# A convolution-attention and mixture-of-experts kernel: pieces of a visit over four PSUM slots, and image 0's sorting spread one operation to a step

## The chip, the cores and the metric

The kernel runs on one core of a Trainium2 chip. The metric is the device time of one execution in microseconds (us). Besides the time of several plain executions there is one execution with the hardware profiler on; its trace gives every instruction's start, duration and wait. Of the engines, TensorE (PE in the profile) multiplies matrices into PSUM, VectorE (DVE) and ScalarE (ACT) work on the elements and copy PSUM results to SBUF, which is called evicting here, GpSimd (POOL) does some element work and issues indirect DMAs, and SyncE (SP) issues most of the other DMAs.

## What is computed

The input x has the shape (2, 256, 56, 56) in float32: two images of 256 channels and N = 3136 positions. All arithmetic is in float32. The reference, cut to what matters:

```python
x = conv_attention(x)              # non-local block over the positions, no softmax, then relu(wy + x)
t = tokens(x)                      # (2, 3136, 256)
t = t + attention(layer_norm(t))   # 4 heads of 64, causal, softmax, projection W_proj
xf = layer_norm(t)
probs = softmax(xf @ gate_w + gate_b)          # 8 experts
top2_vals, top2_idx = top_k(probs, 2)
for e in range(8):                             # hidden width 512
    out += weight(e) * (gelu(xf @ W1[e] + b1[e]) @ W2[e] + b2[e])
x = image(t + out)
```

The reference evaluates every expert for every token; the kernel sorts the tokens by expert and evaluates the two chosen ones.

## The kernel before

**Stages.** The convolution part comes first (to about 92 us). Then layer norm and attention run (92 to about 867 us), image 0 and then image 1. Then the expert stage works through blocks of 128 token places (slots), and the rows are combined and stored.

**Attention.** The queries of an image are cut into 7 bands i of 448, the heads into two pairs hp. A step takes one band, one pair and one block j of 128 keys; there are 200 steps in an image, of some 1.5 us each. A step does `scores` of step n (line 721, into one of two score tiles of two PSUM banks, pool `psc`), the exponential on ACT (729) into a tile `st` (five buffers), on blocks that the diagonal cuts a mask on DVE (731), the running row sums `acc` on DVE (743), and `values` of step n - 3 (761, tile `yp`).

**Visits.** After the last step of a band and pair comes a visit. It does pieces of later work on TensorE: `query_key` (603, evicted by ACT at 611), `value` (618, evicted by ACT at 627; at the end of a segment DVE scales gate columns at 638), `transpose` (589, evicted by ACT at 595) of layer-normed rows, and up to two pairs of output projections (`project_out`, 671, added to the tokens t by DVE at 676, then the mean and variance of the new rows, `stats`, 177 and 178). Every piece takes a PSUM bank from `bank()`, which hands out the two banks of pool `pm` in turn. After the pieces `sum_rows` (785) adds up `acc` over partitions, also in a bank of `pm`.

**The queue.** Beside the visits every step calls `between`, which pulls work from a list of generators, `queue`: on every second step it pulls two pieces. `pull` goes through the generators in their order, and stops at the first that answers True (something was done); one that answers False is passed over, and the next one gets its turn. For each image b there is a generator `tokens(b)`: the output projections of 25 tiles in pairs (which wait for their queries to be finished, and answer "pe" so that a visit takes them up), and then `dispatch(b)`: inverse deviations by Newton steps (1041 to 1053), router and top two experts (1056 and after), rank of each token among its expert's (1122), places, one-hot vectors (1236), and at last, for each tile of 128 tokens, the normalised row `xr` (DVE, 1355; for image 1 also 1361) and two indirect DMAs by POOL that scatter it into `x_slots` (1363). `tokens(0)` then loads the experts' first weights and the first rows. Image 1's generator comes behind image 0's in the queue.

**Experts.** The expert stage takes 102 blocks in its main loop. Each has a transpose (1462), the first product `hidden` (1485), Gelu on ACT (1494), and, three blocks later in order, the second product `outputs` (1504), evicted by DVE (1514, tile `ys`, three buffers). DVE copies the weights of the block two ahead (1473). The blocks run in the order of their slots, image 0's first; blocks 42 to 44 are the first that hold both images' rows. Rows come three blocks to a load, `fetch`: the loads for block n + 6 are issued when block n begins (SP, 1403, and 1415 for the second image's part), and DVE makes them ready three blocks later (1428 to 1439). `fetch` first calls `need(b)`, which pulls the queue without pause until all of image b's rows have been sent. Between blocks `meanwhile` pulls two or three pieces. SP and every other engine run their instructions in the order of the program; `y_slots` (1519) is stored by SP behind `fetch`.

The parts of the code that the change touches:

Of the kernel before, what the change touches and what calls it, by code (L numbers as in the profile page):

```python
# [28 lines left out]
def conv_attn_moe_kernel(  # L29
# [52 lines left out]
    P = 128  # L82
# [429 lines left out]
    def layer1(nm, general):  # L512

        with ExitStack() as whole:
# [4 lines left out]
            bg = pool(whole, "bg", bufs=2)  # L519
            g1 = pool(whole, "g1", bufs=1)  # L520

            def bank(name, shape=(P, 512)):
                return pm.tile(list(shape), F32, tag="m", name=f"{name}_{nm}")

            def centre_gate(place):
# [135 lines left out]
            def project_out(b, qT, done):  # L661

                for first, m, k in pairs():
                    while done() < (first + m - 1) * P + k:
                        yield False
                    yield "pe"
                    for n in range(first, first + m):
                        o = n * P
                        ps = bank(f"pp_{b}_{n}")
                        for c in range(NH):  # L670
                            nc.tensor.matmul(  # L671
                                ps[:k, : C + E], qT[:, c, o : o + k], wpr[:, c, :],
                                start=(c == 0), stop=(c == NH - 1),
                            )
                        t = ts[b][:k, n, : C + E]
                        nc.vector.tensor_tensor(t, t, ps[:k, : C + E], ALU.add)
                        if b == 0:
                            nc.sync.dma_start(out=rest_d[:k, n], in_=t[:, :C])
                    stats(b, first, m, k, bg, f"o{nm}{b}")

                    for _ in range(3 if b else 1):
                        yield True

            def attend(
                b, qT, kT, v, fst, fs, psc, py, visit, between, clock, later, finished
# [145 lines left out]
                for n in range(len(steps) + LAG):  # L831
                    if 0 < n <= len(steps) and steps[n - 1][4]:
                        i, hp = steps[n - 1][:2]
                        visit(i, hp)
                        sum_rows(hp, i)
                    if n < len(steps):
                        i = steps[n][0]
                        between(i, ends[i] - n)

                    late = n >= LAG and steps[n - LAG][3]  # L840
                    if n >= LAG:
                        due(clock[0])
# [161 lines left out]
            def dispatch(b):  # L1004

                t = ts[b]
                tail = chunk(NCH - 1)
                ops = [0]

                def small_piece():  # L1010

# [17 lines left out]
                def wide(ap):  # L1029
# [8 lines left out]
                    small(k, 1).rearrange("p t o -> p (t o)") for k in ("newton_x", "newton_y", "red")  # L1038
                )
                nc.vector.tensor_scalar(x, var, 1e-5, None, ALU.add)  # L1040
                nc.vector.tensor_scalar(
                    y.bitcast(I32), x.bitcast(I32), 1, None, ALU.arith_shift_right
                )
                nc.vector.tensor_scalar(
                    y.bitcast(I32), y.bitcast(I32), -1.0, float(0x5F3759DF), ALU.mult, ALU.add
                )
                yield from small_piece()
                for i in range(4):
                    to = var if i == 3 else y
                    nc.vector.tensor_tensor(z, y, y, ALU.mult)  # L1050
                    nc.vector.tensor_tensor(z, z, x, ALU.mult)
                    nc.vector.tensor_scalar(z, z, -0.5, 1.5, ALU.mult, ALU.add)
                    nc.vector.tensor_tensor(to, y, z, ALU.mult)
                    yield from op()
                    yield from small_piece()
# [294 lines left out]
                for n in range(NCH):  # L1350
                    kk = chunk(n)
                    xr = (scatter_rows[0] if b else bg).tile(
                        [P, width], F32, tag="xr", name=f"xr_{nm}{b}_{n}"
                    )
                    nc.vector.tensor_scalar(
                        xr[:kk, :C], t[:kk, n, :C],
                        t[:kk, n, MEAN : MEAN + 1], t[:kk, n, RSTD : RSTD + 1],
                        ALU.subtract, ALU.mult,
                    )
                    if b:  # L1360
                        nc.vector.tensor_copy(xr[:kk, C:], t[:kk, n, C + E - 2 : SLOT + 1])  # L1361
                    for k in range(2):
                        s = nc.gpsimd.indirect_dma_start(  # L1363
                            out=xds[b],
                            out_offset=bass.IndirectOffsetOnAxis(ap=idxs[b][:kk, k, n : n + 1], axis=0),
                            in_=xr[:kk],
                            in_offset=None,
                            bounds_check=xds[b].shape[0] - 1,
                            oob_is_err=False,
                        )  # L1370
                        group = f"x_slots_{nm}{b}"
                        tc.declare_no_dep(s.ins, group=group, reason="different rows")
                        tc.add_to_no_dep_group(group, s.ins)
                        if b or k:
                            yield True
                    if b == 0:
                        yield False
                sent[b] = True

            def experts(w1s, w2s, b2s, ex, es, ps6, between, need, written, settle, decide):  # L1380
# [538 lines left out]
            else:  # L1919
                fst = pool(att, "fst", bufs=5)  # L1920
                fs = pool(end, "fs", bufs=2, side="right")
                psc = pool(att, "psc", bufs=2, space=PSUM)
                py = pool(att, "py", bufs=1, space=PSUM)
                projections = [project_qkv(b, qT, kT, v, px) for b in range(B)]
                finished = [[0] * NH for b in range(B)]
# [37 lines left out]
                for b in range(B):  # L1963
                    queue.append(tokens(b, qT, lambda b=b: min(finished[b])))

                    def visit(i, hp):

                        now, then = ahead(b, i, hp)
                        for piece in now:
                            piece()  # L1970
                        for _ in range(2):
                            pull()
                            products()
                        for piece in then:
# [12 lines left out]

                    due = attend(
                        b, qT, kT, v, fst, fs, psc, py, visit, between,
# [252 lines left out]
```

## Time and profile before

| | us |
|---|---|
| time, median of 3 runs | 1326.75 (1324.08 to 1327.43) |
| the profiled execution's own time | 1320.51 |
| its span in the trace | 1318.7 |
| TensorE busy | 1269.1 (96%) |
| VectorE busy | 798.3 (61%) |
| ScalarE busy | 610.9 (46%) |
| GpSimd busy | 348.8 (26%) |
| attention: first visit to the first expert block | 92 to 867 |
| first expert block to the end | 867 to 1318.7 |

The mean clock that was granted to TensorE is 0.991 of full speed. Lines in the profile are those of the kernel before. A row of the waits names the waiting instruction and what it was released by, its total in us, the number of waits and the longest one. A row of the timeline has the start in us from the span's start, the duration, the engine, the line, the operation, output and inputs, and in brackets the engine's idle time ahead of it with its releaser. Ends of matmuls are modelled, so that part of a wait can be counted as busy time of the matmul before it; starts are measured.

### The profile page before, as it was taken

Reading aid. Unit: us, or ns where it says so; the run is one execution under the profiler, and the core shown is the slowest. Engines: PE = TensorE matmul, PEld = TensorE weight load, DVE = VectorE, ACT = ScalarE, POOL = GpSimd, SP = SyncE. Lnnn points to the kernel's source line nnn. Section 1 sums busy time; section 2 is a strip of 40 time slices with the busy share of each in tenths; the row PEclk is TensorE's granted clock in tenths of the full one; section 3 lists DMA queues with packets and bytes.
Section 4 is the critical chain, followed back from the end, with each engine's and each line's share of the span. In section 5 each row is a group of like instructions: output and inputs, shape, how many; then the busy total and the mean of one; then the engine's idle time right before and its main releaser. Section 6 shows DMA issues by size and latency. Waiting matters only on the chain.

```text
span 1318.7 us, 28564 instructions
## 1 busy us (share of the span) xinstructions
PE 1269.1 (96%) x10809; PEld 827.2 (63%) x10809; DVE 798.3 (61%) x1673; ACT 610.9 (46%) x1235; POOL 348.8 (26%) x319
## 2 busy tenths in 40 slices
PE   9999999999999999999999999999998999899997
PEld 8875445544444555444444444579987899799996
DVE  1673566666777745756877777754753443355554
ACT  0255555556566544555655455633432333344432
POOL 1113330000002223311126620000066312665551
PEclk9999999999999999999999999999999899999999
DMA  9994100000000001000002243321234343466654
GB/s 317 359 349 129 31 16 24 25 17 16 17 9 8 25 1 37 18 11 9 16 24 81 81 133 95 105 72 53 69 128 147 117 113 94 139 195 193 189 162 132
DMA packets 111074, 123.88 MB, mean 94 GB/s; under 512 B 19703, under 2 KB 100840, under 8 KB 110930
## 3 DMA queue, kind: packets, MB, share of 16 engines
q1 hardware_dynamic: 100130, 95.18, 23.7%
q0 software_dynamic: 9840, 25.67, 5.7%
q8 instruction: 89, 1.46, 0.5%
q10 hardware_dynamic: 960, 1.11, 0.3%
q14 instruction: 55, 0.45, 0.1%
HBM read 62.06 MB, written 61.05 MB: 93 GB/s over the span
## 4 chain that ended last, share of the span: by engine, by line
PE 87%; DVE 6%; ACT 3%; issue 3%; DMA 1%; POOL 0%; SPq 0%; DVEq 0%; ACTq 0%; POOLq 0%
PE sc_f L721 18%; PE yp_f L761 18%; PE ht_f L1485 14%; PE yp_f L1504 13%; PE qk_f L603 7%; PE v_f L618 3%; PE cp L410 3%; DVE acc_f L743 2%; PE gram L317 2%; PE pp_f L671 2%; ACT st_f L729 2%; PE tp_f L1462 2%; PE sp_f L785 1%; PE yo_f L1727 1%; DMA out_dram<-ot_f 1%
## 5 line engine op out<-in xcount | busy, mean ns | idle before, releaser
L729 ACT ACTIVATE st_f<-sc_f 128x896 f32<-128x896 f32 (+5 forms) x400 | 330.4, 840 | 225.0 <-PE sc_f L721 199.3
L743 DVE TENSOR_TENSOR acc_f<-acc_f,st_f 128x896 f32<-128x896 f32 (+5 forms) x372 | 379.9, 1021 | 74.0 <-ACT st_f L729 62.2
L721 PE MATMUL sc_f<-qT_f,kT_f 64*64 64x448 f32 (+6 forms) x3184 | 340.6, 500 | 9.4 <-ACT st_f L729 6.0
L761 PE MATMUL yp_f<-st_f,v_f 64*64 64x448 f32 (+6 forms) x3184 | 339.9, 501 | 3.5 <-DVE st_f L731 2.3
L1494 ACT ACTIVATE g_f<-ht_f,b1b 128x128 f32<-128x128 f32 x408 | 116.5, 370 | 252.0 <-PE ht_f L1485 125.1
L721 PEld LDWEIGHTS sc_f<-qT_f,kT_f 64*64 64x64 f32 x3184 | 121.0, 133 | 164.5 <-issue 124.2
L761 PEld LDWEIGHTS yp_f<-st_f,v_f 64*64 64x64 f32 x3184 | 120.0, 133 | 154.3 <-issue 131.7
L1485 PE MATMUL ht_f<-xT_f,w_f 128*128 128x128 f32 x1632 | 206.4, 280 | 4.5 <-issue 3.6
L1485 PEld LDWEIGHTS ht_f<-xT_f,w_f 128*128 128x128 f32 x1632 | 201.7, 196 | 11.3 <-issue 6.0
L773 POOL TENSOR_TENSOR qT_f<-both_f 128x448 f32<-128x448 f32 x28 | 37.0, 1321 | 503.0 <-ACT both_f L772 503.0
L1363 POOL DMA_INDIRECT x_slots<-xr_f,idx x100 | 110.0, 1100 | 144.0 <-DVE xr_f L1361 100.8
L1473 DVE COPY w_f<-w1s_f 128x1024 f32 x102 | 72.7, 714 | 84.8 <-PE ht_f L1485 37.7
L574 POOL TENSOR_SCALAR xn_f<-t 128x256 f32<-128x256 f32 (+1 forms) x50 | 80.8, 1624 | 155.3 <-PE xp_f L589 66.2
L1525 POOL DMA_INDIRECT y_tokens<-ys_f,to_f x57 | 59.0, 1036 | 126.1 <-DVE ys_f L1514 102.3
L1514 DVE TENSOR_TENSOR ys_f<-yp_f,kT_f 128x128 f32<-128x128 f32 x102 | 29.5, 289 | 102.8 <-PE yp_f L1504 72.8
L603 PE MATMUL qk_f<-px_f,wat 128*128 128x512 f32 (+2 forms) x224 | 88.5, 547 | 0.8 <-ACT px_f L595 0.6
L603 PEld LDWEIGHTS qk_f<-px_f,wat 128*128 128x128 f32 x224 | 40.5, 190 | 46.2 <-issue 41.1
L739 DVE COPY acc_f<-st_f 128x896 f32<-128x896 f32 x28 | 17.9, 641 | 80.1 <-ACT st_f L729 76.3
L1504 PE MATMUL yp_f<-v_f,g_f 128*128 x204 | 62.2, 385 | 2.0 <-issue 1.9
L731 DVE TENSOR_TENSOR st_f<-st_f,keep 128x256 f32<-128x256 f32 (+1 forms) x112 | 45.6, 407 | 30.4 <-ACT st_f L729 29.8
L1504 PE MATMUL yp_f<-px_f,g_f 128*128 x204 | 62.3, 385 | 1.4 <-issue 1.4
L1504 PE MATMUL yp_f<-kT_f,g_f 128*128 x204 | 61.9, 384 | 1.1 <-issue 1.0
(285 smaller groups left out, 1268.4 us busy)
## 6 DMA issues: line engine op xcount, KB each, us to landing
x_slots<-fill SPq DMA_DIRECT2D x1, 8190.0 KB
xb_f<-x_slots SPq DMA_DIRECT2D x60, 130.0 KB
x_slots<-fill SPq DMA_DIRECT2D x1, 7296.0 KB
y_slots<-ys_f SPq DMA_DIRECT2D x57, 128.0 KB
kept<-t SPq DMA_DIRECT2D x2, 3200.0 KB
x<-in_x_dram SPq DMA_DIRECT2D x14, 448.0 KB
rb_f<-inverses SPq DMA_DIRECT2D x56, 112.0 KB
y_f<-y_tokens SPq DMA_DIRECT2D x23, 256.0 KB
```

The source lines that it names most:

```text
L574: nc.gpsimd.tensor_scalar(xn[:k, a], ts[b][:k, n + a, :C], ts[b][:k, n + a, MEAN : MEAN + 1], ts[b][:k, n + a, RSTD : RSTD + 1], ALU.subtr ...
L603: nc.tensor.matmul(ps[:, :w], wat[:, c, d0 : d0 + P], px[:, s % 2, c, :w], start=(c == 0), stop=(c == NH - 1),)
L721: nc.tensor.matmul(ps[h : h + HS, a, c0:W], kT[hp][rows, j * P + h : j * P + h + HS], qT[rows, hp, q0 + c0 : q0 + W], start=True, stop=True,)
L729: nc.scalar.activation(st[:k, :, c0:], ps[:k, :, c0:W], AF.Exp, scale=SCALE)
L743: nc.vector.tensor_tensor(acc[:k, :, c0:], acc[:k, :, c0:], st[:k, :, c0:], ALU.add)
L761: nc.tensor.matmul(yp[a * HS : (a + 1) * HS, h // HS, c0:W], v[hp][h : h + HS, j, a, :HS], st[h : h + HS, a, c0:], start=first, stop=bool( ...
L1363: s = nc.gpsimd.indirect_dma_start(out=xds[b], out_offset=bass.IndirectOffsetOnAxis(ap=idxs[b][:kk, k, n : n + 1], axis=0), in_=xr[:kk], i ...
L1473: nc.vector.tensor_copy(w, w1s[:, :, bass.ds(e, 1), :].rearrange("p c e h -> p c (e h)"))
L1485: nc.tensor.matmul(ht[:, k, :], w[:, c, k * P : (k + 1) * P], xT[:, c, :], start=(c == 0), stop=(c == NH - 1),)
L1494: nc.scalar.activation(g[:, k, :], ht[:, k, :], AF.Gelu, bias=b1bs[b][:, k, i : i + 1])
L1504: nc.tensor.matmul(yp[:, :C], g[:, k, :], w2s[k][:, bass.ds(e, 1), :].rearrange("p e d -> p (e d)"), start=(k == 0), stop=(k == KH - 1),)
L1525: s = nc.gpsimd.indirect_dma_start(out=y_tokens, out_offset=bass.IndirectOffsetOnAxis(ap=to[:, n % GB : n % GB + 1], axis=0), in_=ys, in_o ...
```

## The change

1. `bank()` has a counter `ring` while a visit runs. Its turns are: two from `pm`, then two score tiles from `psc` (one piece to a tile, in its first bank), and so on round. It is cleared before `sum_rows`.
2. For image 0 a visit's projections no longer have the statistics (and their pause) behind them. A new generator, `closer`, goes to the front of the queue and does the mean and variance of one tile for a pull. `dispatch(0)` starts only when all 25 tiles are closed.
3. In `dispatch(0)` every operation yields once, where it yielded once or twice in turn, and each operation of the Newton steps yields by itself, where four went together. Image 1's `dispatch` keeps its yields.
4. After each scattered tile of image 0 the generator answers True where it answered False.
5. A visit no longer pulls the queue; it takes up products twice. `between` pulls one piece on every step, where it pulled two on every second one, except on steps of the first band that the diagonal cuts.

The number of instructions on each engine doesn't change.

```diff
             def bank(name, shape=(P, 512)):
+                turn = ring[0] % 4 if ring else 0
+                if turn > 1:
+                    ring[0] += 1
+                    flat = score_banks[0].tile([P, 2, 512], F32, tag="sc", name=f"{name}_{nm}")[:, 0]
+                    if shape[2:]:
+                        return flat[:, : shape[1] * shape[2]].rearrange("p (a w) -> p a w", a=shape[1])
+                    return flat[:, : shape[1]]
+                if ring:
+                    ring[0] += 1
                 return pm.tile(list(shape), F32, tag="m", name=f"{name}_{nm}")
...
+                    if b == 0:
+                        queue.appendleft(closer(b, first, m, k))
+                        continue
                     stats(b, first, m, k, bg, f"o{nm}{b}")
-                    for _ in range(3 if b else 1):
+                    for _ in range(3):
                         yield True
+                while b == 0 and unclosed[0]:
+                    yield False
+            unclosed = [NCH]
+            def closer(b, first, m, k):
+                for n in range(first, first + m):
+                    stats(b, n, 1, k, bg, f"o{nm}{b}")
+                    unclosed[0] -= 1
+                    yield True
...
-                        between(i, ends[i] - n)
+                        between(i, ends[i] - n, (steps[n][2] + 1) * P > i * W + 1)
...
                 def op():
-                    ops[0] += 1
-                    for _ in range(0 if b else 1 + ops[0] % 2):
+                    if b == 0:
                         yield True
...
                     nc.vector.tensor_tensor(z, y, y, ALU.mult)
+                    yield from op()
                     nc.vector.tensor_tensor(z, z, x, ALU.mult)
+                    yield from op()
                     nc.vector.tensor_scalar(z, z, -0.5, 1.5, ALU.mult, ALU.add)
+                    yield from op()
                     nc.vector.tensor_tensor(to, y, z, ALU.mult)
                     yield from op()
...
                         if b or k:
                             yield True
                     if b == 0:
-                        yield False
+                        yield True
                 sent[b] = True
...
                     def visit(i, hp):
                         now, then = ahead(b, i, hp)
+                        ring.append(0)
                         for piece in now:
                             piece()
                         for _ in range(2):
-                            pull()
                             products()
                         for piece in then:
                             piece()
+                        ring.clear()
-                    def between(i, left):
+                    def between(i, left, cut):
...
                         tick[0] += 1
-                        if tick[0] % 2:
-                            pull(2)
+                        if not cut or i:
+                            pull()
```

More of the change, by code (lines that the diff above doesn't have):

```diff
@@ L520, in layer1 @@
             g1 = pool(whole, "g1", bufs=1)
+            ring, score_banks = [], []
             def bank(name, shape=(P, 512)):
+                turn = ring[0] % 4 if ring else 0
[7 more added lines that the diff above has]
+                    ring[0] += 1
                 return pm.tile(list(shape), F32, tag="m", name=f"{name}_{nm}")
@@ L1007, in dispatch @@
                 tail = chunk(NCH - 1)
-                ops = [0]
                 def small_piece():
@@ L1050, in dispatch @@
                     nc.vector.tensor_tensor(z, y, y, ALU.mult)
+                    yield from op()
                     nc.vector.tensor_tensor(z, z, x, ALU.mult)
+                    yield from op()
                     nc.vector.tensor_scalar(z, z, -0.5, 1.5, ALU.mult, ALU.add)
+                    yield from op()
                     nc.vector.tensor_tensor(to, y, z, ALU.mult)
@@ L1922, in layer1 @@
                 psc = pool(att, "psc", bufs=2, space=PSUM)
+                score_banks.append(psc)
                 py = pool(att, "py", bufs=1, space=PSUM)
```

## The prediction

> **What bounds the kernel now.** I read the page's busy shares first, then TensorE's busy time by stretches, then its waits, then the timeline of the places where it stands still.
>
> ```profile
> PE 1269.1 (96%) x10809; PEld 827.2 (63%) x10809; DVE 798.3 (61%) x1673; ACT 610.9 (46%) x1235; POOL 348.8 (26%) x319
> ...
> PEclk9999999999999999999999999999999899999999
> ...
> PE 87%; DVE 6%; ACT 3%; issue 3%; DMA 1%; POOL 0%; SPq 0%; DVEq 0%; ACTq 0%; POOLq 0%
> ```
>
> TensorE is busy for 96% of the span and holds 87% of the chain that ended last. The change removes no matmul, so it can only win or lose in the 4% in which TensorE stands still (and in its clock). By stretches (start and end, length, TensorE's busy time, ..., granted clock, DMA share, GB/s):
>
> ```profile
> 700.00:860.00 160.00, 152.21 (x1590) 70.47 (x1586) 119.81 (x169) 87.98 (x118) 51.79 (x44) 1.00 0.31 98
> ...
> 958.00:1036.00 78.00, 70.75 (x437) 62.86 (x435) 34.58 (x133) 22.31 (x80) 51.54 (x50) 0.93 0.41 136
> 1036.00:1060.00 24.00, 21.66 (x142) 20.39 (x142) 10.40 (x33) 8.41 (x30) 0.00 (x0) 0.93 0.40 113
> ```
>
> From 150 to 470 us TensorE loses 1% and less; these three lose 5% to 10%. What they share is the POOL scatter of rows (L1363): image 0's in the first, image 1's in the second, its tail in the third. In the last two the clock is 0.93 too. The waits of TensorE in attention (92 to 860 us; total, times, longest):
>
> ```profile
> PE sc_f L721 <- ACT st_f L729: 6.0, 9, 1.2
> PE yp_f L761 <- DVE st_f L731: 2.3, 4, 1.0
> PE xp_f L589 <- DVE t L676: 2.2, 6, 1.1
> ...
> PE sp_f L785 <- ACT kT_f L611: 1.8, 7, 0.3
> ...
> PE sp_f L785 <- ACT v_f L627: 0.9, 3, 0.3
> ...
> PE pp_f L671 <- DVE t L676: 0.6, 1, 0.6
> ```
>
> The last four are what shared banks cost: transposes, row sums and products wait until an older piece of the visit is evicted from one of two banks.
>
> **Part 1: four banks in a visit.** With four slots a piece waits for the eviction four pieces back, not two. That takes away the last four rows, 2.2 + 1.8 + 0.9 + 0.6 = 5.5 us, and three smaller waits of the same kind, 0.4 (sp behind px), 0.2 (sp behind t L638) and 0.2 (qk behind qT): 6.3 in all. The view counts from the modelled end of the piece before. From start to start the same seams are longer: after the usual pitch of a piece, the seven row sums behind kT start 0.28 late where the view says 0.2 to 0.3, the two products at 428.5 start 0.74 late where it says 0.57, the transposes at 544.46 start 1.31 late (0.39 in four other visits) where it says 1.15. Added up over the 30 visits that is 8.6 us. I take -8.6; 6.3 is the lower gain if all evictions stay on time. The two last visits (822 and 861 us) hold only two products and then row sums; nothing changes for them. What may eat the gain: a score tile that a piece has used must be evicted before the next scores. Between lie the row sums and values (0.52 and 0.8 us) and at most one 0.58 copy, so I cost it at nothing; if ACT were late there, up to 0.3 per visit, 8 us, would come back. That leaves 0 to -8.6.
>
> [...]
>
> **Part 2: sorting one operation a step, variances later.** DVE is in order, and a lump of sorting operations ahead of a mask makes TensorE wait. The timeline shows it (DVE, then TensorE, at 556 us):
>
> ```profile
> 556.03 0.20 DVE L1053 TENSOR_TENSOR t<-newton_y_f,red_f 128x25 f32<-128x25 f32 x1
> ...
> 556.27 0.37 DVE L1056 TENSOR_TENSOR lg_f<-t 128x200 f32<-128x200 f32 x1
> ...
> 557.62 0.42 DVE L731 TENSOR_TENSOR st_f<-st_f,keep 128x256 f32<-128x256 f32 x1
> ...
> 558.10 0.77 PE L761 MATMUL yp_f<-st_f,v_f 64*64 64x320 f32 x8 [0.96 <-DVE st_f L731]
> ```
>
> All four waits of the row "yp_f behind st_f L731" lie between 553 and 637 us, where image 0 is sorted. One operation of 0.2 to 0.4 us a step of 1.5 us, in place of three to eight in one step, should take most of them: start to start they cost 3.6 us, of which I take -2. The variance pieces (0.41 + 0.18 a tile, 25 tiles, 14.7 us of DVE) leave the visits and lie in steps, where DVE is 61% busy. If they fall on masks, they cost one operation's 0.6 some six times, +4; if they help all evictions, -4. Range -4 to +4. The new order of the sort keeps the same operations; image 0's scatters still go one tile in two steps, so the stutter of 700 to 770 us stays. w1's eight loads on SP come 5 to 13 steps later and still end some 40 steps (60 us) ahead of the experts: nothing.
>
> Attention: -8.6 - 2 = -10.6, bounds -15 and +2.
>
> **Part 3: what moves into the expert stage.** After each scatter tile of image 0 the generator now reports work done, so that a pull stops there and image 1's generator is not reached until image 0 is sorted. In the order of instructions image 1's projections then begin after step 375 and not after step 308; three pairs (about 5.5 us of TensorE) move from visits into the expert blocks. TensorE pays them either way: 0. But the rest of image 1's chain moves five blocks later: Newton from block 13 to 18, ranks from 17 to 22, the first scatter from 21 to 26. The block that needs it doesn't move. At block 36 the rows of blocks 42 to 44 are fetched, and a fetch first pulls everything unsent. Before, 44 of 50 scatters have run when block 36 begins; after, by the order, about 29. The other 21 go in one burst. Its pitch and what follows (POOL, SP, DVE):
>
> ```profile
> 1033.60 0.91 POOL L1363 DMA_INDIRECT x_slots<-xr_f,idx  x1 [0.30 <-issue]
> ...
> 1034.82 0.99 POOL L1363 DMA_INDIRECT x_slots<-xr_f,idx  x1 [0.30 <-issue]
> ...
> 1037.51 1.44 SPq L1403 DMA_DIRECT2D xb_f<-x_slots  x3
> ...
> 1044.74 0.15 DVE L1428 TENSOR_TENSOR eq_f<-xb_f,sid 128x3 f32<-128x3 f32 x1
> ...
> 1045.21 0.96 DVE L1439 TENSOR_TENSOR xb_f<-xb_f,xo_f 128x768 f32<-128x768 f32 x1
> ```
>
> The burst takes 21 x 1.28 = 26.9 us. From the last scatter's end (1035.81) to usable rows it took at most 1046.17 - 1035.81 = 10.4 us (DVE came to it late), and at least up to the end of the loads' issue (1039.4) plus 1.4 of DVE, 5.0. I take 7.7. DVE waits at L1428 for those rows, and behind it in its queue stands the weight copy L1473 (0.7) of block 41. So block 41 begins 26.9 + 7.7 + 0.7 = 35.3 us after block 36. Before it was 1051.60 - 1028.32 = 23.3. The difference is +12.0; five blocks of 3.73 us fill 18.7 of the 35.3, and TensorE stands for about 16 us. SP waits at L1403 just as long, and the stores of blocks 33 to 35 queue behind it; they are needed by the eviction of block 36, which stands behind L1428 anyway.
>
> Against that: scatters make blocks stutter. The 15 blocks from 955.76 to 1028.32 took 72.6 us where 15 x 3.73 is 56.0: 16.6 lost to 45 scatters, 0.37 each. Fifteen fewer lie ahead of block 36: -5.5; those of the burst stutter inside the wait. And after the stand the clock is at half: such a dip lasted 3.4 us (974, 1039) or 6.8 (1018, 1148) in this trace, so 1.7 to 3.4 lost: +2.5. Sum +12.0 - 5.5 + 2.5 = +9; with 5.0 or 10.4 for the rows, stutter unrelieved or as counted, +4 to +17.
>
> [...]
>
> **Sum.** -10.6 + 9 = -1.6 us against the profiled execution's own 1320.5 us (span 1318.7), so 1319; that execution ran 6.2 us under the median of the runs shown, 1326.75, so I forecast 1325.
>
> **The rivals.**
> *Stall cheaper than counted (faster).* The rows land within 5.0 us, the stutter ahead of block 36 falls by more than its share, and all bank waits go: -13 + 4, about -9: 1318, range 1313 to 1322. For it: TensorE has no other work that the change delays. Against it: SP's loads are in order behind the burst.
> *The forced burst at block 36 (slower).* Image 1's late sort costs its full +13 to +17, while attention gives -4 because DVE is late with the variances: +9 to +13, so 1336 to 1340. It decides from the point at which the last scatter ends more than the slack of before after block 36: rows were usable at 1046.2 and first needed near 1049.7, 3.5 us. 21 scatters in place of 6 pass it by far; what is open is the size, and whether attention pays it back.
> *The change doesn't do what it says.* The bank waits come back as waits for score tiles behind ACT at the group's first scores (that row is 6.0 us already): attention -2, experts +9, +7: 1334.
>
> **Chances.** Forecast, within 0.3% (4 us, about what a measurement of this kernel can tell from no change): 0.37, its own range 1322.7 to 1330.7. Cheaper stall: 0.30. Burst at full price: 0.25. Waits only moved: 0.08. So faster 0.30, same 0.37, slower 0.33. The range goes from the faster rival's 1313 to the slower one's 1340.
>
> **What would show it.** Part 1: the rows "xp_f behind t L676" and "sp_f behind kT_f" (or v_f) gone from the waits, and "sc_f behind st_f" not above 6. Part 2: "yp_f behind st_f L731" under 1 us. Part 3: 20 or so L1363 back to back after block 36 begins, a stand of TensorE of 12 to 20 us before the rows of block 42 are used, and a clock dip after it. I am wrong if POOL has sent more than 40 scatters when block 36 begins (no stall, about -10), if block 41 begins over 42 us after block 36, or if attention doesn't get shorter by 6 us beyond the three pairs that leave it.

## The result, and the profile after

The changed kernel takes 1328.99 us (median of 22 runs, 1323.95 to 1332.53), the kernel before beside it 1326.12 (22 runs, 1319.96 to 1329.81). The ratio is 1.0024, with a 95% interval of 1.0013 to 1.0036: the change makes the kernel 0.24% slower. The forecast was 1325, a gain of 1.6 us and so nearly no change; its sign was wrong. The profiled execution took 1324.13 us, its span is 1322.4 (before: 1320.51 and 1318.7).

The page of the kernel after, its busy shares, the clock and the chain:

```profile
PE 1267.7 (96%) x10809; PEld 828.5 (63%) x10809; DVE 794.9 (60%) x1673; ACT 610.2 (46%) x1235; POOL 349.9 (26%) x319
...
PEclk9999999999999999999999999999998699899999
...
PE 90%; DVE 3%; issue 3%; ACT 2%; another core or an unknown queue 1%; DMA 1%; POOL 0%; DVEq 0%; ACTq 0%; SPq 0%; POOLq 0%
```

The busy shares are within a point of those of before. What is new is one place: an 8 and a 6 in the row of the clock, in the slices from 992 to 1058 us. TensorE's waits in attention (92 to 860 us) in the kernel after:

```profile
PE sc_f L746 <- ACT st_f L754: 5.2, 7, 1.2
...
PE sp_f L810 <- DVE t L687: 1.1, 2, 0.6
PE sp_f L810 <- DVE t L649: 1.1, 2, 0.9
...
PE yp_f L786 <- DVE st_f L756: 0.3, 1, 0.3
```

The rows "xp_f behind t", "sp_f behind kT_f", "sp_f behind v_f" and "pp_f behind t" are gone, DVE's late masks have fallen from 2.3 to 0.3, and the scores don't wait longer (5.2, before 6.0). The first of the two rows of `sp_f` is the two last visits, of which the prediction said that nothing changes: 0.57 us each, before as after. In the second 0.9 us came back, at one visit, behind the gate columns (the row was 0.2 before). The small wait of `sp_f` behind `px_f`, which was to go, stayed (0.5, before 0.4). Stretches of the kernel after (columns as in the prediction); the second is the scatter before block 36, the third goes from block 36 to block 41:

```profile
700.00:860.00 160.00, 150.41 (x1572) 70.74 (x1565) 116.54 (x157) 89.20 (x123) 53.49 (x45) 1.00 0.33 106
966.00:1009.00 43.00, 40.23 (x254) 35.70 (x253) 22.01 (x90) 13.88 (x50) 27.62 (x27) 0.96 0.42 136
1009.00:1054.00 45.00, 25.76 (x134) 21.09 (x134) 13.11 (x48) 6.98 (x25) 23.64 (x24) 0.70 0.38 120
1054.00:1140.00 86.00, 86.00 (x600) 81.24 (x599) 34.94 (x97) 30.99 (x111) 23.35 (x25) 1.00 0.38 113
```

In the third TensorE is busy for 25.8 of 45 us, at a clock of 0.70, beside 24 scatters. The starts of the blocks' first product in the timeline divide the span (us):

| | first block at | blocks 0 to 21 | 21 to 36 | 36 to 41 | 41 to the end |
|---|---|---|---|---|---|
| before | 867.0 | 88.7 | 72.6 | 23.3 | 267.1 |
| after | 853.5 | 90.5 | 65.2 | 45.2 | 268.0 |
| difference | -13.5 | +1.8 | -7.4 | +21.9 | +0.9 |

The differences add up to the spans' +3.7. Of the -13.5, some 5.5 are the three pairs of projections, which come back in blocks 0 to 21; 8.0 is what attention gained. What is won ahead of block 36 is more than lost from block 36 to 41. There the timeline shows (POOL, TensorE, SP, ACT, DVE):

```profile
1036.94 0.37 PE L1514 MATMUL ht_f<-xT_f,w_f 128*128 128x128 f32 x1 [1.57 <-issue]
...
1037.52 0.91 POOL L1392 DMA_INDIRECT x_slots<-xr_f,idx  x1 [0.30 <-issue]
...
1038.74 0.91 POOL L1392 DMA_INDIRECT x_slots<-xr_f,idx  x1 [0.30 <-issue]
...
1039.03 0.37 PE L1514 MATMUL ht_f<-xT_f,w_f 128*128 128x128 f32 x1 [1.73 <-issue]
...
1041.86 0.37 PE L1514 MATMUL ht_f<-xT_f,w_f 128*128 128x128 f32 x1 [1.05 <-issue]
...
1042.53 1.58 SPq L1432 DMA_DIRECT2D xb_f<-x_slots  x3
...
1043.37 1.14 ACT L1523 ACTIVATE g_f<-ht_f,b1b 128x128 f32<-128x128 f32 x4 [23.75 <-remote]
...
1048.22 0.96 DVE L1468 TENSOR_TENSOR xb_f<-xb_f,xo_f 128x768 f32<-128x768 f32 x1
...
1052.45 0.38 PE L1491 MATMUL tp_f<-ident,xb_f 128*128 128x128 f32 x2
...
1054.40 1.84 PE L1514 MATMUL ht_f<-xT_f,w_f 128*128 128x128 f32 x15
```

The burst is there: 26 scatters stand back to back from 1005.99 to 1039.65, 23 of them after block 36 has begun. The forecast had TensorE run through block 40 beside them and then stand. Instead it crawls. From the second half of block 37 on its matmuls come with pauses, and in the first product of block 38 it gets one in 1.4 to 2.1 us, where 0.11 us is its pitch at a granted clock of 1.00 (16 in 1.78 us from 1046.94 on). It waits there for nothing that the profile shows ("issue"); one more wait of 3.8 us, ahead of block 38, is behind DVE, which itself started late. In what follows, to starve TensorE means this. Block 38 starts at 1026.50, block 39 only at 1046.94, after the burst.

The last three rows decide what block 41 waited for. The rows of block 42 are usable at 1049.18 (1048.22 + 0.96). TensorE comes to their transposes at 1052.45, 3.3 us later, and it has worked without a pause since 1043.26. So here block 41 waited for TensorE's own crawl; the rows, late as they were, were ready before TensorE came to them.

### The profile page after: what moved, and what is told of

Its sections match the earlier page's. It is cut to its first block, busy times and chain, and to the rows that moved or that the text cites. A ratio compares the mean times of both kernels' runs of the same rounds, so it can differ in the third digit from the quotient of the medians.

```text
span 1322.4 us, 28535 instructions
## 1 busy us (share of the span) xinstructions
PE 1267.7 (96%) x10809; PEld 828.5 (63%) x10809; DVE 794.9 (60%) x1673; ACT 610.2 (46%) x1235; POOL 349.9 (26%) x319
## 4 chain that ended last, share of the span: by engine, by line
PE 90%; DVE 3%; issue 3%; ACT 2%; another core or an unknown queue 1%; DMA 1%; POOL 0%; DVEq 0%; ACTq 0%; SPq 0%; POOLq 0%
PE sc_f L746 19%; PE yp_f L786 19%; PE ht_f L1514 14%; PE yp_f L1533 13%; PE qk_f L614 7%; PE cp L410 3%; PE v_f L629 3%; PE pp_f L682 3%; PE gram L317 2%; PE tp_f L1491 2%; ACT st_f L754 2%; DVE acc_f L768 1%; PE sp_f L810 1%; PE yo_f L1756 1%
## 5 line engine op out<-in xcount | busy, mean ns | idle before, releaser
L1502 DVE COPY w_f<-w1s_f 128x1024 f32 x102 | 72.6, 712 | 95.5 <-PE ht_f L1514 35.2
L1554 POOL DMA_INDIRECT y_tokens<-ys_f,to_f x57 | 58.3, 1023 | 125.8 <-DVE ys_f L1543 100.3
L1533 PE MATMUL yp_f<-w2s_f,g_f 128*128 x204 | 62.0, 385 | 1.9 <-issue 1.7
```

Source lines behind the costliest of these rows:

```text
L1502: nc.vector.tensor_copy(w, w1s[:, :, bass.ds(e, 1), :].rearrange("p c e h -> p c (e h)"))
L1533: nc.tensor.matmul(yp[:, :C], g[:, k, :], w2s[k][:, bass.ds(e, 1), :].rearrange("p e d -> p (e d)"), start=(k == 0), stop=(k == KH - 1),)
L1554: s = nc.gpsimd.indirect_dma_start(out=y_tokens, out_offset=bass.IndirectOffsetOnAxis(ap=to[:, n % GB : n % GB + 1], axis=0), in_=ys, in_o ...
```

## The experiments

Each set of runs was on a chip of its own, and each ratio is against the kernel before on the same chip. The kernel before took 1316 to 1326 us beside the result and in three of the sets, and 1287 to 1288 in two. A time without a ratio is of a single execution, the profiled one.

**Which part makes the loss.** Theory: image 1 is sorted five blocks later, so that a long run of scatters stands in front of the rows of block 42 and starves TensorE. Rivals: late rows alone; the moved projections; bank waits that only moved. The first set takes the parts apart.

```diff
 # false_again: the changed kernel
                     if b == 0:
-                        yield True
+                        yield False
                 sent[b] = True
 # true_alone: the kernel before with that one line as in the changed kernel
 # ring_alone: the kernel before with bank()'s ring of the changed kernel
 # pull_more: the changed kernel
-                    pull(3 if sorting or worked[0] >= MIXED else 2, every=True)
+                    pull(5 if sorting else 3 if worked[0] >= MIXED else 2, every=True)
```

> The changed kernel, but image 0's generator answers False again after a scattered tile, so that a pull goes on to image 1's projections. Theory, starved TensorE: the loss of the change is one long run of back-to-back scatters at block 36, in which TensorE's instructions come one in 1.4 to 2.1 us, and it comes only because image 1 is sorted five blocks later. Here it is sorted as early as before, so the 8.0 us that attention gained stay: about 1318, ratio 0.994. Rival, moved projections: the three pairs that went into the expert blocks make those blocks dearer; they go back too, so 0.994 as well. Rival, late rows: the same. If the other parts cost something in the expert stage, 1.000 or more.

Measured: 1306.89 us against 1318.89, ratio 0.9915 (0.9889 to 0.9941). Blocks 36 to 41 take 20.6 us.

> The kernel before with nothing but the four slots in a visit. Starved TensorE and late rows alike: the order outside the visits is that of before, so only the bank waits go: -6 to -8.6 us, 1318 to 1320, ratio 0.994. Rival, waits only moved: the waits come back at the score tiles, 1.000.

Measured: 1307.78, ratio 0.9926 (0.9902 to 0.9949). The first block begins at 858.4 where it was 867.0 before: -8.6, the number of Part 1. That the two agree to a tenth is luck: the two profiles are of different sets, and a second profile of the kernel before has its first block at 871.3. TensorE's waits in attention; the rows of `xp_f` and `pp_f`, and those of `sp_f` behind `kT_f` and `v_f`, are gone:

```profile
PE sc_f L732 <- ACT st_f L740: 6.1, 6, 3.3
PE yp_f L772 <- DVE st_f L742: 2.6, 5, 1.0
...
PE sp_f L796 <- DVE t L687: 1.1, 2, 0.6
```

> The kernel before with nothing but True in place of False after image 0's scattered tile. Starved TensorE: 20 scatters in one run at block 36, +11 us as in the changed kernel, so about 1337, ratio 1.008, and single matmuls 1.4 us apart in the run. Late rows (the step of the prediction): blocks 36 to 40 run beside the scatters and only then TensorE stands: +9, ratio 1.007, with the stand in one piece before block 41. Moved projections: the same pairs move, +5 to +11, but with the loss in blocks 1 to 15.

Measured: 1333.57, ratio 1.0116 (1.0090 to 1.0143), +15 us for one word, more than the +9 to +11 expected. Blocks 0 to 21 take 2.8 us more than in the profile of before for 5.5 of moved projections, so these cost nothing beyond their own time. Blocks 36 to 41 take 38.4 us. Both mechanisms show: waits for "issue", and one stand behind the rows of block 42 (TensorE's waits from 1023 to 1062 us):

```profile
PE tp_f L1462 <- DVE xb_f L1439: 5.0, 1, 5.0
PE ht_f L1485 <- issue: 3.2, 5, 0.8
```

> The changed kernel, with five pieces of image 1's sorting pulled in a block in place of three. All rows are sent by order in block 32, four blocks ahead of their first use, but the scatters stand back to back from block 24, all 50 of them. Late rows: no stand at block 41, about 10 us faster than the changed kernel, 1318. Starved TensorE: after the first 7 or so of the run TensorE loses about 1.2 us to each scatter, some 40 x 1.2 = 50 us in place of the 28 lost there now: about 20 us slower than the changed kernel, 1350.

Measured: 1337.24, ratio 1.0156 (1.0130 to 1.0182), about 17 us slower than the changed kernel's 1.0024. The rows are in time: blocks 36 to 41 take 18.7 us, five times 3.73. But blocks 21 to 36 take 100.3 us where 56.0 is usual. The stretch of its scatters:

```profile
960.00:1044.00 84.00, 61.01 (x303) 48.94 (x301) 31.73 (x130) 16.06 (x56) 50.51 (x50) 0.76 0.35 116
```

So starving exists without late rows, at 44 us for 50 scatters, where the expectation had about 50. The moved projections are out as the cause: they have moved here too, and blocks 36 to 41 lose nothing. (The whole run holds a second loss: block 20 takes 11.9 us for a wait of 6.5 behind DVE, for the ranks of the sort that is pulled faster.)

**The sort without the slots, and a spread sort.** The second set was on a chip where the kernel before took 1287.18.

```diff
 # sort_alone: false_again without  ring.append(0)
 # fast_sort_25: false_again
-                    pull(3 if sorting or worked[0] >= MIXED else 2, every=True)
+                    pull((2 + worked[0] % 2 if placed[1] else 6) if sorting else 3 if worked[0] >= MIXED else 2, every=True)
 # fast_sort_3: the same with 3 in place of 2 + worked[0] % 2
 # paced: the changed kernel, behind each scatter
+                        if b:
+                            nc.gpsimd.memset(fill, 0.0)
+                            nc.gpsimd.memset(fill, 0.0)
```

> The changed kernel without the four slots and with False again: only the sorting one operation a step and the later variances are left. The first expert block began at 867.0 us before, at 858.5 with the four slots alone and at 854.0 with slots and sorting, so the sorting is worth about 4 us: ratio 0.997 against before. If it needs the slots to pay (a shorter visit), 1.000.

Measured: 1284.59, ratio 0.9977 (0.9965 to 0.9989): 3 us.

> The changed kernel with False again behind image 0's scattered tiles, and with image 1's sorting pulled six pieces to a block until its places are known, then two and three in turn. The scatters begin in block 18 (21 before) and take 2.5 a block, 3.2 us of POOL in 3.73, so that gaps break them into runs of 8 and fewer; 2 are left for block 36. Starved TensorE: the runs so far lost nothing up to 8, 2 to 3 us of standing at 10 to 12, 7 at 18 and 19 at 26, so that most of the 18 us that blocks 21 to 41 lose in the kernel with False again go: about 10 us faster than that one, ratio 0.983 to 0.986. If the loss goes with the number of scatters and not with their runs (rival), it stays: 0.9915.

Measured: 1278.21, ratio 0.9936 (0.9922 to 0.9950).

> As the run with two and three in turn, but three pieces to a block throughout: scatters from block 18, 3.84 us of POOL in a block of 3.73, so that they stand back to back. All are sent by block 33, three blocks earlier. Starved TensorE: runs grow to 12 and more, no better than the kernel with False again, ratio 0.99 to 1.0. Rival, late rows: as good as the run with two and three, since the rows are there in time.

Measured: 1278.37, ratio 0.9931 (0.9918 to 0.9945). This is what the rival said, but for a reason that was not expected: all 50 scatters stand in one run from 932 to 999 us, and TensorE loses nothing to them. The stretch of blocks 21 to 41:

```profile
941.00:1019.00 78.00, 78.00 (x540) 72.44 (x539) 37.69 (x121) 28.70 (x103) 45.11 (x44) 1.00 0.49 155
```

TensorE is busy for 78.00 of 78.00 us at full clock. So starving is not a property of the program alone; on this chip it is absent. Both sorts also pay about 7.5 us for a wait of their own: block 15 takes 11.4 us, with 6.0 of waiting for the ranks behind DVE.

> The changed kernel with two small POOL memsets of an idle tile behind each scatter of image 1, which leaves out nothing: the pitch of the scatters goes from 1.28 to about 1.9 us. Starved TensorE by back-to-back scatters: the blocks run on at 3.73 us beside the scatters, block 40 begins near 1022, and then TensorE stands in one piece until the last of 50 x 1.9 us has been sent, so block 41 begins near 1070 (1054 in the changed kernel); matmuls 1.4 us apart are gone. If the scatters starve it whatever lies between them (rival), single matmuls come 1.4 to 2 us apart for the whole 95 us and no stand in one piece is seen.

Measured: 1340.36. Block 40 begins at 1010.8 and block 41 at 1080.9, with one wait of 64.7 us behind the rows; block 41 begins 12.0 us after the last scatter's end. On this chip that shows late rows, and nothing on starving.

**The same on one chip.** The third set repeats four kernels on a chip where the kernel before takes 1324.44.

> The kernel before once more, for its profile beside the others of this set. In the set with the sorting at a faster rate it took 1287 us where it took 1319 and 1326 in the others, and there no run of up to 50 scatters starved TensorE. Starved TensorE: where this run takes 1319 and more, blocks 21 to 36 lose 15 us and more to runs of scatters; where it takes about 1287 they lose under 4 us.

Measured: 1324.75; blocks 21 to 36 take 71.3 us (15.3 over fifteen times 3.73), 36 to 41 take 22.4.

> The changed kernel once more. Where the kernel before takes 1319 and more: TensorE starved from block 37 on, ratio 1.002 as before. Where it takes about 1287: blocks 36 to 40 run at 3.73 us, and TensorE stands in one piece of some 15 to 18 us until the rows of block 42 are ready (the late rows of the prediction), which is +12 us less what attention gains, 8 us: ratio 1.003. If nothing but starving made the loss, it falls to 0.994 there.

Measured: 1326.72, ratio 1.0026 (1.0009 to 1.0043). Blocks 36 to 41 take 48.7 us, the first block begins at 853.6 again (871.3 in the kernel before on this chip). Block 39 begins at 1050.61, and from there TensorE runs at 3.73 us a block up to block 41: the crawl, not the rows, was what block 41 waited for here too.

> The changed kernel with False again. Where the kernel before takes 1319 and more: 0.9915 as measured. Where it takes about 1287: the four slots and the sorting pay 8 to 13 us, and the last scatters end as before, ratio 0.990 to 0.994.

Measured: 1310.01, ratio 0.9901 (0.9879 to 0.9923).

> The kernel with False again and a sort of six pieces a block, then two and three in turn. Where the kernel before takes 1319 and more and long runs of scatters starve TensorE: shorter runs, 0.983 to 0.986, better than False again alone by some 8 us. Where it takes about 1287: 0.9936 as measured, no better than False again, since no run starves TensorE there.

Measured: 1310.55, ratio 0.9893 (0.9869 to 0.9918). Blocks 21 to 41 take 86.6 us (95.2 with False again), but blocks 0 to 21 take 96.4 (88.5): what the spread order wins, its own wait for the ranks takes back. The expected 8 us stayed out for that reason.

**What starves TensorE.** The fourth set was on a chip where the kernel before takes 1316.16: a control, the paced kernel, and one whose bound leaves out image 1's rows beyond the first 128 places.

```diff
 # dropped: the changed kernel; y_tokens is zeroed at the start
-                            bounds_check=xds[b].shape[0] - 1,
+                            bounds_check=127 if b else xds[b].shape[0] - 1,
 # two_a_block: false_again
-                    pull(3 if sorting or worked[0] >= MIXED else 2, every=True)
+                    pull(4 if not projected[1] else (2 if placed[1] else 3) if sorting else 3 if worked[0] >= MIXED else 2, every=True)
```

> The changed kernel, as the control for the two runs behind it on the same chip. Where the kernel before takes 1319 and more, TensorE crawls from block 37 on while 26 scatters stand back to back, and block 41 begins 45 to 49 us after block 36. Where the kernel before takes about 1287, it stands in one piece before block 41 and that distance is 34 to 36 us (late rows alone).

Measured: 1317.79. Blocks 36 to 41 take 37.9 us, with the crawl (blocks 38 to 40 alone take 26.0). That is less than the 45 to 49 expected; the long run had 22 scatters here, of which 20 were left for block 36.

> The changed kernel with two small POOL memsets behind each scatter of image 1, now to be read against the control. If back-to-back issue starves TensorE: blocks 26 to 40 run at about 3.73 us on this chip too, with one stand of 60 us and more before block 41. If it is the scatters' number whatever lies between them: single matmuls come 1.4 us apart beside all of them.

Measured: 1352.70. Blocks 26 to 40 take 3.93 us each, as on the other chip (3.93), and no wait for "issue" is left there. TensorE's waits from 950 to 1090 us have one row:

```profile
PE tp_f L1495 <- DVE xb_f L1472: 64.3, 1, 64.3
```

The timeline beside block 39 (a scatter, two memsets of 0.3, the next scatter 2.1 us later):

```profile
1008.88 0.97 POOL L1393 DMA_INDIRECT x_slots<-xr_f,idx  x1 [0.50 <-issue]
...
1009.85 0.33 POOL L1405 MEMSET fill<- 128x260 f32 x1
...
1009.88 1.95 PE L1518 MATMUL ht_f<-xT_f,w_f 128*128 128x128 f32 x16
...
1010.24 0.32 POOL L1406 MEMSET fill<- 128x260 f32 x1
...
1010.99 0.97 POOL L1393 DMA_INDIRECT x_slots<-xr_f,idx  x1 [0.43 <-issue]
```

On a chip that starves, the same scatters with a pause between them don't starve TensorE (3.93 us a block; blocks 38 to 40 took 26.0 us in the control), so in these two runs it is how densely they stand and not their number. Whether the pause counts or the lower rate, this run doesn't separate.

> The changed kernel, in which the bound of image 1's scatters is set to the first 128 places, so that POOL issues all 50 but nearly all rows are dropped and not written; the rows' sums over image 1 are left out with them, and the table that they would fill is zeroed at the start. If TensorE is starved by the rows that the DMA engines write: the blocks beside the burst run at 3.73 us and only the rows' lateness is left, block 41 34 to 36 us after block 36. If it is what POOL does to issue them: the crawl of the control stays, 45 us and more.

Measured: 1321.21. It does not decide. Blocks 36 to 40 took 16.7 us beside a run of 20 (34.2 in the control), but blocks 32 to 34 took 17.7 us, where 7.5 is usual, beside a run of 12.

> False again, four pieces a block while image 1's projections run, three while it is sorted, and then two: the scatters begin in block 14, take 2.56 us of POOL in a block of 3.73, so that each pair is followed by a gap, and 6 are left for block 36. Starved TensorE where the kernel before takes 1319 and more: no runs, so the 15 to 18 us that blocks 21 to 41 lose with False again mostly go, ratio 0.978 to 0.983. Rival, the loss goes with the number of scatters: 0.990 as with False again. Where the kernel before takes about 1287: 0.990.

Measured: 1297.87 against 1316.16, ratio 0.9851 (0.9828 to 0.9875). Blocks 21 to 41 here, and those of the kernel before (from the profile beside the prediction, not of this set):

```profile
941.00:1027.00 86.00, 86.00 (x596) 80.00 (x595) 39.83 (x129) 32.44 (x115) 45.68 (x43) 1.00 0.41 134
```

```profile
956.00:1052.00 96.00, 86.42 (x539) 77.64 (x538) 43.03 (x162) 28.17 (x100) 51.54 (x50) 0.93 0.41 134
```

The first is the run with two a block: TensorE busy throughout, at full clock, beside 43 scatters, mostly in pairs (the longest run in the stretch has 6). The kernel before loses 9.6 of 96 us there and has a clock of 0.93. The forecast of 0.978 to 0.983 was missed. The likely reason is a wait of 6.1 us in block 1 (products behind t L687, behind the DMA of the scaling rows); blocks 1 and 2 take 18.3 us.

The last set was on a chip where the kernel before takes 1288.13.

```diff
 # two_or_three: false_again
+                    pull(3 if not projected[1] else (2 + (worked[0] % 4 == 0) if placed[1] else 3) if sorting else 3 if worked[0] >= MIXED else 2, every=True)
```

> As the run with two a block, but three pieces a block until the scatters begin (four before, which put an addition of projected rows behind a DMA round trip in blocks 1 and 2 and cost TensorE about 12 us there), and three in every fourth block of the scatters: they begin in block 16, and 6 are left for block 36. Starved TensorE where the kernel before takes 1312 and more: no runs over 6, and most of the 12 us back, ratio 0.977 to 0.981 (two a block: 0.985). Where the kernel before takes about 1287: 0.987 to 0.990. If the stand in blocks 1 and 2 stays: 0.985.

Measured: 1276.11, ratio 0.9911 (0.9893 to 0.9928), where 0.987 to 0.990 was expected. The wait in block 2 is still 5.3 us.

> The changed kernel with image 1's rows dropped, a second time: rows over the first 128 places are not written, and the rows' sums over image 1 are left out. In the first such run the blocks beside the long run of scatters took 16.7 us from block 36 to 40 (34.2 in the control), but two blocks beside a run of 12 before it took 17.7 us where 7.5 is usual. If it is the written rows that starve TensorE: no block longer than 6 us from 26 to 40. If it is POOL's issuing, blocks of 8 us and more beside a run of 10 and more again.

Measured: 1295.82, no block of 26 to 40 over 5 us. But the kernel before takes 1288 us on this chip, much as on the one where a run of 50 with all its rows cost nothing, so this tells nothing on the written rows. It does show what late rows cost by themselves:

```profile
1024.29 0.91 POOL L1392 DMA_INDIRECT x_slots<-xr_f,idx  x1 [0.30 <-issue]
...
1026.61 1.44 SPq L1432 DMA_DIRECT2D xb_f<-x_slots  x3
...
1032.05 0.96 DVE L1468 TENSOR_TENSOR xb_f<-xb_f,xo_f 128x768 f32<-128x768 f32 x1 [1.58 <-DMA y_slots<-ys_f]
...
1033.11 0.66 PE L1491 MATMUL tp_f<-ident,xb_f 128*128 128x128 f32 x2 [21.06 <-DVE xb_f L1468]
...
1033.56 1.06 PE L1533 MATMUL yp_f<-px_f,g_f 128*128 x2
...
1036.78 1.39 PE L1514 MATMUL ht_f<-xT_f,w_f 128*128 128x128 f32 x11
```

Block 36 began at 994.75. The last scatter ends 30.5 us later, the rows are transposed 7.9 us after that, and block 41 begins another 3.7 us later, because one block's second product stands between, at half pace (two of its matmuls in 0.85 us, from 1033.56 to 1034.41; in the kernel after, at a granted clock of 1.00, in 0.43 from 1052.67 on): 42.0 us in all. From the last scatter to block 41 that is 11.6 us; in both paced runs, where the rows are written, it is 12.0.

## Why the prediction was wrong

The step that failed is the burst in Part 3. Its cost was added up too small, and it rested on an overlap that did not take place: blocks 36 to 40 were to run at 3.73 us beside the scatters. From block 36 to 41 the forecast had +14.5 us (+12.0, and +2.5 for the clock); it was +21.9, and +26.3 in the third set (22.4 to 48.7). Those 7 us and more turn the sign of a forecast gain of 1.6.

**Part 1 (four slots, -8.6) was right.** The slots alone bring the first block 8.6 us forward, and the ratio 0.9926 is -9.8 us (-6.7 to -12.9). The waits that it was added up from stood in the trace of before with 6.3 us by the view, and the four rows that make 5.5 of them are gone in the run with the slots alone.

**Part 2 (sorting one operation a step, -2) had the right sign.** Alone it measures -3 us; DVE's late masks fell from 2.3 to 0.3 us. For both parts together attention gained 8.0 us in the profiles beside the result and 12.1 in those of the third set (17.6 less the 5.5 of the moved pairs); the forecast was 10.6. Its bounds of -15 and +2 don't follow from the parts, which give -12.6 and +4.

**Part 3: the moved projections (0) were right, the burst (+9) was mis-sized.** Undoing the one word brings the ratio from 1.0024 (on its own chip) to 0.9915, and from 1.0026 to 0.9901 on one chip, and the word alone makes 1.0116: it costs 14 to 17 us. (The changed kernel's order had its first block between 848.2 and 853.6 us in six profiles on the chips that starve, so single profiles don't settle 3 us there.) Term by term:

- *21 scatters at 1.28 us, 26.9.* It was 23 at 1.32: 30.4 us from the start of block 36 to the end of the last one, +3.5. 27 had begun when block 36 did, not 29.
- *Rows ready 7.7 us after the last scatter.* 7.9 up to their transposes where nothing disturbs it, +0.2. In the changed kernel it was 9.5, since SP's load began 2.9 us after the last scatter (1.7 in the kernel before), and DVE had an eviction to do ahead of the rows.
- *Then 0.7 for block 41's weights.* This is an error of order: the transposes of block 42 and a whole second product come before block 41 in TensorE's queue. At a granted clock of 1.00 they take 1.95 us (1052.45 to 1054.40 above), +1.3.
- *A dip of the clock, +2.5.* In the second run with dropped rows the same instructions took 3.7 us at half pace, where 1.95 is usual, so the dip costs about 1.7, -0.8.
- *Blocks 36 to 40 run beside the scatters.* They do not, on the chips that starve: block 39 began 37.7 us after block 36, when the burst was over.
- *Stutter ahead of block 36, -5.5.* It was -7.4.

With the first four terms put right, late rows alone hold block 41 until 42.0 us after block 36, as measured in the second run with dropped rows, in which nothing starved, where the forecast had 37.8 (35.3 and 2.5). The changed kernel took 45.2, and 48.7 in the repeat, because TensorE, starved during the burst, still had blocks 39 and 40 ahead of it when the burst was over. The two costs lie over each other and don't add up: late rows alone would make some 19 of the +21.9, and the crawl, which ended last, sets the rest. The control shows how much this varies: with 20 scatters left, and a crawl, block 41 came 37.9 us after block 36.

The whole difference of the profiles, +3.7 us where -1.6 was forecast, is then: attention -8.0 (forecast -10.6), blocks 0 to 21 without the moved pairs -3.7 (0), blocks 21 to 36 -7.4 (-5.5), blocks 36 to 41 +21.9 (+14.5), the rest +0.9 (0). The burst is off by 7.4; the next miss to the slow side, attention's 2.6, is not borne out by the third set, where attention gained more than forecast.

The trace of before held a hint: beside a run of 12 scatters blocks 34 and 35 took 14.3 us where 7.5 is usual, and the prediction spread the loss evenly, 0.37 us on each scatter, where this run alone lost 6.8 us, 0.57 on each.

**The rivals.** Of the slower one the place and the point of decision were right (it passes the slack of 3.5 us by far), its second half wrong: attention paid in full. Of the prediction's own signs of being wrong one came true: block 41 began over 42 us after block 36 (45.2). "The waits only moved" is out, and so is the cheaper stall.

**A better version.** Undoing the word beats both kernels (0.9915 and 0.9901). Two scatters a block make 0.9851 on another chip that starves, where undoing the word alone was not run; the intervals (up to 0.9875, and from 0.9879 and 0.9889) don't overlap. Where long runs don't starve, the sorts that begin earlier make 0.9911 to 0.9936, with intervals that overlap; undoing the word alone was not run on those chips.

## What to carry to other kernels

When an edit delays a chain of work whose deadline stands fixed in the program, count what is left at the deadline and follow the queue of the bound engine past it, instruction by instruction, up to the one whose start is wanted. A word that tells a scheduler "done" or "pass on" moves whole chains behind it; the order of instructions shows it before any run. And a cost seen beside runs of one kind of work should be plotted against the length of a run before it is averaged. When two costs of one cause lie over each other, the one that ends last sets the time, and the difference between two runs does not split into their sum.

## What was not expected of the hardware

Back-to-back scatters from POOL starve TensorE on some chips and not on others. (No chip served for two sets, so that a chip's own nature and its state at the time are not told apart.) Added up from the gaps between TensorE's matmuls in the traces of before and after, its standing beside one run of image 1's scatters (and 4 us after it) was 0 to 0.1 us for runs of 6 and 8, 2.0 to 2.9 for runs of 10 and 12, and 19.2 for the one of 26, the clock not counted. The loss is not fixed by the length: the repeat of the changed kernel lost 13.2 us beside its run of 26, and the kernel before with the one word lost 0.9 beside a run of 14 and 7.0 beside one of 18. On the chip where the kernel before takes 1287 us a run of 50 cost nothing (TensorE busy for 78.00 of 78.00 us beside 44 of them). On that with 1288 it cost nothing either (no block of 26 to 40 over 5 us), but there only a run of 50 with its rows dropped was tried.

Image 1's scatters are not all that differs between the chips. On the two with 1287 and 1288 the scores wait 1.1 us in all behind ACT in attention, where the other sets show 2.7 to 8.4, and from block 41 to the end every kernel takes 257 to 258 us, where the other sets show 267 to 271. No run shows what makes these two differences.

On the chip with 1316 a pause of some 1.1 us between two scatters took the starving away (no wait for "issue" from 950 to 1090 us), and so did sending them mostly in pairs with a gap (TensorE busy for 86.00 of 86.00 us beside 43). The engines that take up TensorE's products start late in such a run too: in the changed kernel the first products of blocks 36 and 37 end at 1011.30 and 1015.03 by the model, and ACT begins its Gelu on them at 1017.75 and 1043.37. Whether the written rows or POOL's issuing makes it, or something else in the chip, no run shows: the one run on a starving chip that dropped the rows went both ways.
